# The last projections and the first kept pair by block products, in the second pass of a three-pass fp32 layer

## The chip, the cores and the metric

The kernel runs on one core of a Trainium2 chip. The metric is the device time in microseconds; of several executions the median counts. The profile is one further execution, recorded by the hardware profiler. Engines are named as in the profile: PE is the matrix engine (TensorE), DVE the vector engine, ACT the scalar engine, POOL GpSimd, SP the engine whose queue issues most DMAs.

## What is computed

The reference is a "macaron" layer on x of 4 x 1024 x 1024, all in fp32: a feed-forward part, an attention part, the same feed-forward part again, each on the layer-normed x and added to it.

```python
x = x + 0.5 * ffn(layernorm(x))
x = x + attention(layernorm(x))
x = x + 0.5 * ffn(layernorm(x))
...
def ffn(x):                                   # x: 4096 tokens of 1024
    dots = softmax(x @ centroids.T / 0.1)     # 64 clusters
    hits = dots > 0.01
    dense = x @ weight.T + bias
    return where(any(hits, axis=1)[:, None] & any(hits, axis=0)[assignments][None, :], dense, 0)
```

The attention mixes the heads of one token only (`bsdh,bseh->bsde`), and the repeat of k and v over the heads lets the 32 query heads be summed to 8, so that q, k and v together are 768 columns. Which columns of a feed-forward output count is known only when all tokens have been through the gate (`dots`), so each feed-forward part is finished one pass later than it is begun.

## The kernel before, in words

The 4096 tokens are 32 tiles of 128 rows (`NT = 32`). There are three passes over the tiles, each written out by hand in the order of the program; every engine takes its own instructions in that order. The first pass does the first feed-forward product. The second pass, the loop `for s in range(NT + 5)` at the middle of the file, adds it, does the attention, and begins the second feed-forward part. The third does the rest of the products and writes the output.

**The second pass as a pipeline.** Step s works on several tiles at once: it projects tile s to q, k and v, does the attention's small products of tile b = s - 2, adds the attention's result of g = s - 3 on POOL (`second_added`) and norms that tile for the second feed-forward part, transposes f = s - 4 into xT, and gates a = s - 5 (`gate_2`, eight matmuls of 320 columns that give the last 256 output columns and the 64 gate logits). On DVE the order within a step is: the maximum and the subtraction of the scores (L886, L888), the thresholds of the gates (`gated`, four small instructions per tile, L408 to L414), the transpose and the sums of the exponentials (L897 to L910), the moments of tile g (`moments`, `normed`, L162 to L173), and then whatever evicts the products of this step, and the attention's output o (L929, L931).

**Block products.** `project` multiplies one tile by 768 columns of wqkv: 2 x 8 matmuls of 384 columns. `project_two` does the same for two tiles with Strassen's scheme in Winograd's form: seven products of 4 matmuls of 384 columns where the plain way takes eight. The steps of PAIRED = range(4, 30) use it; a generator, `two`, is advanced five products in the even step and two in the odd one. Its sums of weights (`qts`) lie in the first 768 columns of wc, where W.T of the feed-forward part lay in the first pass; W.T was saved to DRAM (`wtd`) and is brought back by four DMAs from SP, blocks 0 and 1 in step 29, blocks 2 and 3 in step 30. Tiles 0 to 3, 30 and 31 use `project`.

The feed-forward products of a pair of tiles are `winograd`: seven products in the order 1, 5, 2, 6, 7, 3, 4. Product 6 is accumulated **onto** product 1's PSUM bank (`onto=u`, L303), and product 4 onto product 7's (`onto=y`, L326). Product 1's bank is also read by DVE before that, since product 1 alone, with the bias, belongs to one quarter of the output:

```python
        u = prod(1, a11, w11)
        add(ca[:, 0], u, b1)
...
        prod(6, s2, t2, onto=u)
```

In the same way `add(cb[:, 1], y, ca[:, 1])` reads product 7 ahead of product 4. The sums of weights `ts` lie in wqkv (`blocks(wqkv)`), so that they can be written only when the projections are done; the sums of tokens `ss` are made by POOL.

The last six tiles (`KEPT`, 26 to 31) stay on chip for the third pass, and some of their products are done in the second pass's last five steps, which have no projection. Before the change tiles 26 and 27 are done by `rest` in steps 32 and 33, one tile per step (2 x 8 matmuls of 384 columns, each half evicted by DVE with the bias), with two of the four weight sums on DVE after each; tiles 28 and 29 are done by `winograd` in steps 34 and 35. In step 34 its first three products are called ahead of `moments`.

**The gates' book.** `gate_2(a)` leaves the logits in es[a]; at the end of the step ACT takes the exponential; `gates_used` in a later step empties es and applies the thresholds. In a paired odd step two tiles are gated, a and f (a + 1), except where the next step is not paired. In a step that is not paired the last lines are `elif has(a) and a not in es: gate_2(a)`.

PSUM holds four banks for products and transposes (`bank`, tag mm), and four that hold the scores and the attention's output in turn (tag att).

Of the kernel before, what the change touches and what calls it, by code (L numbers as in the profile page):

```python
# [33 lines left out]
KEPT = 6  # L34
LAST = 2 * HALF, (EMB + NCL) // 2 - HALF
GATED = range(8, 28)
PAIRED = range(4, 30)
WARM = 16
ROWS = 26

# [2 lines left out]
def kernel(  # L43
# [39 lines left out]
    nc = tc.nc  # L83
    xf = x.flatten_outer_dims()
    of = out.flatten_outer_dims()
    NT = xf.shape[0] // P
# [20 lines left out]
    for base, sign in ((0, 1), (HKV - 1, -1)):  # L107
        nc.gpsimd.affine_select(
            out=tq,
            in_=tq,  # L110
# [9 lines left out]
    wc = const.tile([P, KT, EMB + NCL], F32, name="wc")  # L120
# [14 lines left out]
    xt, dt_, xT = {}, {}, {}  # L135
# [79 lines left out]
    def ffn_part(src, i, dst, name, biased=True):  # L215


        lo, hi = PARTS[i]
        p = product(src, wc, lo, hi, f"ff_{name}_{i}")
        hi = min(hi, EMB)  # L220
        if biased:
            nc.vector.tensor_tensor(dst[:, lo:hi], p[:, : hi - lo], brow[:, lo:hi], ALU.add)
        else:
            nc.scalar.copy(dst[:, lo:hi], p[:, : hi - lo])
        return p[:, hi - lo : hi - lo + NCL] if i == 2 else None

    def rest(t):

        for i in range(2):
            ffn_part(xT[t], i, dt_[t], f"3_{t}")  # L230
        del xT[t]

    def blocks(wts, lo=0, n=HALF):

        return [
            wts[:, 4 * i : 4 * i + 4, lo + h * n : lo + (h + 1) * n] for i in (0, 1) for h in (0, 1)
        ]

    def weight_sums(ws, ts, engines):

        w11, w12, w21, w22 = ws
        t1, t2, t3, t4 = ts
        sums = (t1, w12, w11), (t2, w22, t1), (t3, w22, w12), (t4, w21, t2)
        for engine, (o, p, q) in zip(engines, sums):
            engine.tensor_tensor(o, p, q, ALU.subtract)
            yield
# [214 lines left out]
    def first_added(t):  # L461
        masked(dt_[t], t, 0, mask)
        nc.gpsimd.tensor_tensor(xt[t], xt[t], dt_.pop(t), ALU.add)  # L463
# [6 lines left out]
    with (  # L470
# [5 lines left out]
        ts = [stage.tile([P, 4, HALF], F32, tag=f"ws{i}", name=f"ws{i}") for i in range(4)]  # L476
# [286 lines left out]
    with (  # L763
# [129 lines left out]
        def weighted(s, t, between=lambda: None):  # L893


            st = attn.tile([P, NBLK, 4, D], F32, tag="stt", name=f"stt{t}")
            nc.vector.transpose(  # L897
                st.rearrange("p b t d -> p (b t d)"), s.rearrange("p b t e -> p (b t e)")
            )
            between()  # L900
            sm = small.tile([P, 2, 4, 4], F32, tag="asm", name=f"asm{t}")
            nc.vector.tensor_reduce(
                sm.rearrange("p m i t -> p i m t"),
                s.rearrange("p (i m) t e -> p i m t e", m=2),
                AX.X,
                ALU.add,
            )
            rs = small.tile([P, D], F32, tag="rs", bufs=3, name=f"rs{t}")
            nc.vector.transpose(rs, sm.rearrange("p m i t -> p (m i t)"))
            nc.vector.reciprocal(rs, rs)  # L910
            return st, rs
# [44 lines left out]
        def has(t):  # L956
            return 0 <= t < NT
# [13 lines left out]
        def gate_2(a):  # L971
            if a not in dt_:
                dt_[a] = row(f"d3_{a}")
            es[a] = gate(ffn_part(xT[a], 2, dt_[a], f"3_{a}", biased=a >= FIRST_KEPT), a, 1)

        def gates_used():
            for a in sorted(es):
                gated(es.pop(a), a, 1)
                if a < FIRST_KEPT:
                    store_2(a)  # L980

        for s in range(NT + 5):
            b, g, f, a = s - 2, s - 3, s - 4, s - 5
            paired, odd = s in PAIRED, s % 2 == 1
            if has(s + 4):
                load_2(s + 4)
            for i in {PAIRED.stop - 1: (0, 1), PAIRED.stop: (2, 3)}.get(s, ()):

                nc.sync.dma_start(out=blocks(wc)[i], in_=wtd[i])
            if has(b):  # L990
                sc = scores(qkv[b][0], kd.pop(b), b)
            if has(b):
                nc.scalar.activation(sc, sc, AF.Exp, scale=QK_SCALE)
            if paired:
                if not odd:
                    two = project_two(s, s + 1, ss2)
                next(two)
            if has(s + 1) and s + 1 not in xT2:
                xT2[s + 1] = transposed(xn2.pop(s + 1), f"2_{s + 1}")
            if has(s - 1):  # L1000
                kd[s - 1] = keys(qkv[s - 1][0], s - 1)
            if has(g):
                second_added(ot.pop(g), rs.pop(g), g)
            if g >= 0 and g < FIRST_KEPT:
                nc.gpsimd.dma_start(out=y2[g], in_=xt[g])
            if odd or not paired:
                gates_used()
            if 3 <= s <= 4:
                next(qsums)
            if has(s + 2):  # L1010
                normal = sums_normed(xt[s + 2], f"2_{s + 2}")
                next(normal)
            if paired and not odd:
                next(two)
            if has(b):
                st, rs[b] = weighted(sc, b, lambda: next(two) if paired and odd else None)
            if paired and not odd:
                first_added(s + 3)
                next(two)
            if has(s + 2):  # L1020
                xn2[s + 2] = next(normal)
            if paired and not odd:
                next(two)
            if paired and odd and s + 1 in PAIRED:
                gate_2(a)
                xT[f] = transposed(xn3.pop(f), f"3_{f}")
            if paired and (not odd or s + 1 not in PAIRED):
                fo = attend(st, qkv.pop(b)[1], b)
            if s == NT + 2:
                dt_[a] = row(f"d3_{a}")  # L1030
                steps = winograd(s - 6, s - 5, ss, ts, None, 3)
                for _ in range(3):
                    next(steps)
            if has(g):
                mv = moments(xt[g], f"3_{g}")

            def between():
                if has(s + 3) and s + 3 in dt_:
                    first_added(s + 3)
                if has(g):  # L1040
                    xn3[g] = normed(xt[g], mv, f"3_{g}")

            if paired:
                if not odd:
                    next(two)
                between()
            elif has(s):
                flat[s] = project(xT2.pop(s), s, between)
            else:
                between()  # L1050
                k = s - NT
                if k < 2:
                    rest(s - 6)
                    if k == 0:
                        sums = weight_sums(blocks(wc), ts, [nc.vector] * 4)
                    for _ in range(2):
                        next(sums)
                if k > 2:
                    load_xT(k - 3)
                if 2 <= k < 4:  # L1060
                    for _ in range(1 if k == 2 else 3):
                        next(steps)
            if paired and odd:
                qkv[s] = rearranged(flat.pop(s), s)
            if has(b) and b in qkv:
                fo = attend(st, qkv.pop(b)[1], b)
            if s in flat:
                qkv[s] = rearranged(flat.pop(s), s)
            if has(b):
                ot[b] = returned(fo, b)  # L1070
            if has(s - 1):
                qkv[s - 1] = (qkv[s - 1][0], values(qkv[s - 1][1], s - 1))
            if has(f) and f in xn3:
                xT[f] = transposed(xn3.pop(f), f"3_{f}")
            if odd and s + 1 in PAIRED:
                xT2[s + 2] = transposed(xn2.pop(s + 2), f"2_{s + 2}")
                ss2 = token_sums(xT2, s + 1, s + 2, "2q")
            if 1 <= s <= 3:

                for _ in range(2 if s == 1 else 1):  # L1080
                    next(held[s // 2])
                i = {1: NT - 4, 3: NT - 2}.get(s)
                for i in (i, i + 1) if i else ():
                    nc.sync.dma_start(out=d1[i], in_=dt_.pop(i))
            if s == 1:
                next(qsums)
            if s == NT + 1:
                ss = token_sums(xT, f - 1, f, 2)
                asg = load_assigned()
            if s == NT + 3:  # L1090
                hot = one_hot(asg)
            if paired:
                if odd:
                    gate_2(f if s + 1 in PAIRED else a)
            elif has(a) and a not in es:
                gate_2(a)
            for i in sorted(es) if odd or not paired else ():
                es[i] = gate_exp(es[i], i, 1)
# [118 lines left out]
```

## Time and profile before

| what | value |
|---|---|
| median of three runs | 1326.33 us (1325.13 to 1327.94) |
| the profiled execution, its own time | 1330.44 us |
| span in that profile | 1328.7 us |
| PE busy | 1304.5 us, 98% |
| DVE, ACT, POOL busy | 875.3, 495.3, 583.3 us |
| granted PE clock | 0.995 |

Every fp32 matmul of the program leaves two records in the profile (16 matmuls of a tile's projection are 32 records), and records overlap, so a stage's length is read from the starts of the merged lines and not from the mean duration of a record. In the timelines below a line gives start, length, engine, source line, operation, output and inputs, count, and in brackets the idle time before it and what ended it. A step of the second pass begins on PE with its scores (sc, L877).

### The profile page before, as it was taken

How to read it: one execution, taken by the hardware profiler on the slowest of the kernel's cores; microseconds unless marked ns; L12 is line 12 of the kernel's file. 1: busy time of each engine (PE TensorE's matmuls, PEld its weight loads, DVE VectorE, ACT ScalarE, POOL GpSimd, SP SyncE). 2: the span in 40 equal slices, each digit the busy share in tenths (PEclk: the TensorE clock that was granted, in tenths of full speed). 3: DMA queues.
4: the chain of work that ended last, by engine and by line, in shares of the span. 5: the costliest groups of instructions: out<-in, count | busy, mean ns of one | idle time of the engine just before them, and what ended most of it. 6: DMA issues, size and time to landing. Idle time of an engine off the chain costs nothing.

```text
span 1328.7 us, 22771 instructions
## 1 busy us (share of the span) xinstructions
PE 1304.5 (98%) x8726; PEld 842.6 (63%) x8726; DVE 875.3 (66%) x1789; ACT 495.3 (37%) x821; POOL 583.3 (44%) x448
## 2 busy tenths in 40 slices
PE   8998899999999999999999999999999999999998
PEld 7664577676776665666666666666666655555554
DVE  4574555655546458788888888878867448555556
ACT  4342132332310335666666666666653200000000
POOL 2631123412112238666666666666632336634440
PEclk8999999999999999999999999999999999999999
DMA  8376766677524055566666656656551346755532
GB/s 294 75 155 147 157 148 140 148 178 189 118 95 183 20 160 179 153 192 197 199 185 198 199 165 198 198 186 187 158 171 29 97 140 218 250 194 176 177 117 81
DMA packets 296301, 214.25 MB, mean 161 GB/s; under 512 B 240064, under 2 KB 255168, under 8 KB 296192
## 3 DMA queue, kind: packets, MB, share of 16 engines
q1 hardware_dynamic: 278240, 164.78, 45.4%
q0 software_dynamic: 8736, 30.68, 6.3%
q10 hardware_dynamic: 9216, 17.33, 3.6%
q8 instruction: 69, 1.13, 0.4%
q14 instruction: 40, 0.33, 0.1%
HBM read 127.77 MB, written 84.96 MB: 160 GB/s over the span
## 4 chain that ended last, share of the span: by engine, by line
PE 89%; DVE 5%; issue 2%; ACT 2%; DMA 1%; SPq 1%; ACTq 0%; DVEq 0%
PE st L284 38%; PE qs L801 18%; PE ff L212 16%; PE tp L205 4%; PE la L348 4%; PE pq L212 4%; PE sc L877 2%; PE po L919 2%; DVE d L275 1%; DVE bn L162 1%; SPq L490 1%; PE tpw L558 1%; DMA scd<-sc 0%; DVE best L414 0%; DMA x<-in_L_attn_x_dram 0%
## 5 line engine op out<-in xcount | busy, mean ns | idle before, releaser
L212 PE MATMUL ff<-wc,xT 128*128 128x320 f32 (+1 forms) x768 | 218.7, 439 | 1.0 <-ACT xT L206 0.6
L212 PEld LDWEIGHTS ff<-wc,xT 128*128 128x128 f32 x768 | 144.1, 191 | 63.8 <-issue 1.2
L284 PE MATMUL st<-wc,xT 128*128 128x384 f32 x496 | 170.4, 487 | 0.0
L257 POOL TENSOR_TENSOR ts<-xT 128x512 f32<-128x512 f32 x31 | 42.2, 1361 | 291.3 <-DVE xT L509 95.3
L275 DVE TENSOR_TENSOR d<-st,d 128x384 f32<-128x384 f32 x157 | 85.9, 549 | 106.6 <-PE st L284 105.5
L857 POOL TENSOR_TENSOR kd<-qk,tmask 128x1024 f32<-128x1024 f32 x32 | 60.6, 1893 | 162.5 <-DMA qk<-qkvd 159.5
L284 PEld LDWEIGHTS st<-wc,xT 128*128 128x128 f32 x496 | 93.3, 191 | 60.3 <-issue 1.2
L284 PE MATMUL st<-ws,ts 128*128 128x384 f32 x384 | 131.2, 487 | 0.1
L284 PE MATMUL st<-wqkv,ts 128*128 128x384 f32 x360 | 121.3, 486 | 0.0
L162 DVE BATCH_NORM_STATS2 bn<-x 128x6 f32<-128x512 f32 x132 | 84.2, 680 | 34.9 <-DMA x<-in_L_attn_x_dram 33.3
L801 PE MATMUL qs<-wc,ts_2q 128*128 128x384 f32 x312 | 106.2, 490 | 0.0
L463 POOL TENSOR_TENSOR x<-x,d 128x1024 f32<-128x1024 f32 x32 | 75.4, 2356 | 68.9 <-DVE d L452 52.8
L452 DVE SCALAR_TENSOR_TENSOR d<-d,qsel,mask 128x1024 f32<-128x1024 f32 (+2 forms) x68 | 104.0, 1530 | 0.1
L284 PEld LDWEIGHTS st<-wqkv,ts 128*128 128x128 f32 x360 | 68.3, 190 | 48.1 <-issue 0.8
L284 PEld LDWEIGHTS st<-ws,ts 128*128 128x128 f32 x384 | 71.1, 190 | 43.4 <-issue 1.6
L165 ACT ACTIVATE mv<-mv,eps 128x1 f32<-128x1 f32 x66 | 19.4, 295 | 205.0 <-DVE mv L164 198.4
L284 PE MATMUL st<-wc,ts 128*128 128x384 f32 x248 | 86.7, 494 | 4.0 <-DVE d L275 4.0
L206 ACT COPY xT<-tp 128x512 f32<-128x512 f32 x138 | 73.2, 581 | 32.2 <-PE tp L205 31.3
L801 PEld LDWEIGHTS qs<-wc,ts_2q 128*128 128x128 f32 x312 | 58.2, 190 | 40.5 <-issue 2.6
L275 DVE TENSOR_TENSOR d<-st,brow 128x384 f32<-128x384 f32 x93 | 51.2, 550 | 43.3 <-PE st L284 43.1
L948 POOL TENSOR_TENSOR x<-x,ot 128x1024 f32<-128x1024 f32 x32 | 78.0, 2439 | 2.5
L509 DVE STREAM_TRANSPOSE xT<-xb 128x1024 f32<-128x1024 f32 x27 | 33.6, 1245 | 67.2 <-ACT xb L505 52.9
(143 smaller groups left out, 2294.2 us busy)
## 6 DMA issues: line engine op xcount, KB each, us to landing
x<-in_L_attn_x_dram SPq DMA_DIRECT2D x64, 512.0 KB, 4.4
d<-d SPq DMA_DIRECT2D x64, 512.0 KB, 4.4
out_dram<-x ACTq DMA_DIRECT2D x30, 512.0 KB, 4.7
xb<-in_L_attn_x_dram SPq DMA_DIRECT2D x108, 128.0 KB, 4.9
y<-x POOLq DMA_DIRECT2D x26, 512.0 KB, 3.1
xTd<-xT POOLq DMA_DIRECT2D x26, 512.0 KB, 5.5
xT<-xTd SPq DMA_DIRECT2D x26, 512.0 KB, 5.0
x<-y SPq DMA_DIRECT2D x26, 512.0 KB, 5.2
```

The source lines that it names most:

```text
L162: nc.vector.bn_stats(st[:, i, :], src[:, i * 512 : (i + 1) * 512])
L205: nc.tensor.transpose(tp[:, j, :], xn[:, k * P : (k + 1) * P], ident)
L206: nc.scalar.copy(t_[:, 4 * h : 4 * h + 4, :], tp)
L212: nc.tensor.matmul(p, src[:, k, :], wts[:, k, lo:hi], start=(k == 0), stop=(k == KT - 1))
L275: nc.vector.tensor_tensor(out, ps, other, ALU.add)
L284: nc.tensor.matmul(ps, src[:, k, :], wts[:, k, :], start=(k == 0 and onto is None), stop=(k == 3), skip_group_check=onto is not None,)
L348: nc.tensor.matmul(ps, src[:, k, :], wts[:, k, :], start=(k == 0 and onto is None), stop=(k == 3), skip_group_check=onto is not None,)
L452: nc.vector.scalar_tensor_tensor(d[:, sl], d[:, sl], qsel[which][:, t : t + 1], mask[:, sl], ALU.mult, ALU.mult)
L463: nc.gpsimd.tensor_tensor(xt[t], xt[t], dt_.pop(t), ALU.add)
L801: nc.tensor.matmul(ps, src[:, k, :], wts[:, k, :], start=(k == 0 and onto is None), stop=(k == 3), skip_group_check=onto is not None,)
L857: nc.gpsimd.tensor_tensor(kd, qk[:, :, D:].unsqueeze(2).to_broadcast([P, NBLK, 4, D]), tmask.unsqueeze(1).unsqueeze(3).to_broadcast([P, NB ...
L948: nc.gpsimd.tensor_tensor(xv, xv, ov, ALU.add)
```

## The change

PAIRED is extended to range(4, 32): tiles 30 and 31 are projected by `project_two`. Steps 29 and 31 thereby get the form of the other odd steps. W.T comes back in step 31: blocks 1 and 0 at its start, blocks 3 and 2 after the sums of the exponentials. `rest` is deleted; tiles 26 and 27 are done by `winograd`, four products in step 32 and three in step 33, after `moments` and `normed`. Their sums of tokens, and the first two sums of weights, are put at the end of step 31; the other two sums of weights follow the four products in step 32.

```diff
-PAIRED = range(4, 30)
+PAIRED = range(4, 32)
...
-    def rest(t):
-
-        for i in range(2):
-            ffn_part(xT[t], i, dt_[t], f"3_{t}")
-        del xT[t]
...
+        def returns(*some):
+
+            for i in some:
+                nc.sync.dma_start(out=blocks(wc)[i], in_=wtd[i])
...
-            for i in {PAIRED.stop - 1: (0, 1), PAIRED.stop: (2, 3)}.get(s, ()):
-
-                nc.sync.dma_start(out=blocks(wc)[i], in_=wtd[i])
+            if s == NT - 1:
+                returns(1, 0)
...
                 st, rs[b] = weighted(sc, b, lambda: next(two) if paired and odd else None)
+            if s == NT - 1:
+                returns(3, 2)
             if paired and not odd:
-                first_added(s + 3)
+                if has(s + 3):
+                    first_added(s + 3)
...
-            if paired and odd and s + 1 in PAIRED:
+            if paired and odd:
                 gate_2(a)
                 xT[f] = transposed(xn3.pop(f), f"3_{f}")
-            if paired and (not odd or s + 1 not in PAIRED):
+            if paired and not odd:
                 fo = attend(st, qkv.pop(b)[1], b)
...
                 between()
                 k = s - NT
                 if k < 2:
-                    rest(s - 6)
-                    if k == 0:
-                        sums = weight_sums(blocks(wc), ts, [nc.vector] * 4)
+                    for _ in range(4 - k):
+                        next(steps)
+                if k == 0:
                     for _ in range(2):
                         next(sums)
...
+            if s == NT - 1:
+                ss = token_sums(xT, f - 1, f, 2)
+                steps = winograd(f - 1, f, ss, ts, None, 3)
+                sums = weight_sums(blocks(wc), ts, [nc.vector] * 4)
+                for _ in range(2):
+                    next(sums)
...
             if paired:
                 if odd:
-                    gate_2(f if s + 1 in PAIRED else a)
+                    gate_2(f)
             elif has(a) and a not in es:
                 gate_2(a)
```

## The prediction

> **What bounds the kernel now.** First the page's busy times and the waits of PE, then the order of PE and of DVE in the steps that the change touches. The page, and PE's waits from 900 to 1130 us (us in total, times, longest):
>
> ```profile
> PE 1304.5 (98%) x8726; PEld 842.6 (63%) x8726; DVE 875.3 (66%) x1789; ACT 495.3 (37%) x821; POOL 583.3 (44%) x448
> ```
> ```profile
> PE tp L205 <- ACT xT L206: 1.8, 1, 1.8
> PE ff L212 <- DVE d L275: 0.5, 1, 0.5
> ```
>
> PE works through; after 1060 us it has no wait at all. So what PE gains or loses in steps 29 to 35 reaches the end in full. PE's timeline of steps 29 to 32:
>
> ```profile
> 952.01 2.79 PE L801 MATMUL qs<-wc,xT 128*128 128x384 f32 x8
> ...
> 964.50 0.66 PE L205 MATMUL tp<-ident,xn 128*128 128x128 f32 x4 [1.78 <-ACT xT L206]
> 964.99 10.58 PE L212 MATMUL pq<-wqkv,xT 128*128 128x384 f32 x32
> ...
> 999.68 1.07 PE L877 MATMUL sc<-kd,qk 32*32 32x128 f32 x64
> 1000.68 10.59 PE L212 MATMUL ff<-wc,xT 128*128 128x384 f32 x32
> 1011.20 1.07 PE L919 MATMUL po<-stt,vt 32*32 32x128 f32 x64
> 1012.19 1.09 PE L205 MATMUL tp<-ident,xn 128*128 128x128 f32 x8
> 1013.12 4.47 PE L212 MATMUL ff<-wc,xT 128*128 128x320 f32 x16
> ```
>
> Prices from starts: a projection or a tile of `rest` takes 10.5 us, one product of four matmuls a quarter of that, 2.63; a gate 4.4 (1013.12 to 1017.53), scores 1.0, attention's output 1.0, a transpose 0.93. Now DVE in the same step 32:
>
> ```profile
> 1000.78 1.23 DVE L886 TENSOR_REDUCE amx<-sc 128x32 f32<-128x1024 f32 x1
> ...
> 1007.35 1.22 DVE L162 BATCH_NORM_STATS2 bn<-x 128x6 f32<-128x512 f32 x2
> ...
> 1009.50 0.55 DVE L222 TENSOR_TENSOR d<-ff,brow 128x384 f32<-128x384 f32 x1
> 1011.30 0.56 DVE L222 TENSOR_TENSOR d<-ff,brow 128x384 f32<-128x384 f32 x1 [1.25 <-PE ff L212]
> 1011.78 1.75 DVE L245 TENSOR_TENSOR wqkv<-wc 128x1536 f32<-128x1536 f32 x1
> ```
>
> The reader is to see the lag: the first half of tile 26 is ready on PE at 1005.9, but DVE evicts it at 1009.50, since the scores, thresholds, exponentials and moments stand ahead of it. The eviction ends at 1010.05, 10.4 us after the step's start at 999.68. In step 33 it is the same (1027.90 against 1017.53). Before the change that lag costs nothing: the other half goes to another bank.
>
> **What the Trainium skill says.** "TensorE: Matmul & The Clock Gate", Step-by-step: what each phase is for: matmuls stay in program order, only weight loads are pulled ahead; so one matmul that waits holds all behind it. The trace agrees: in the first pass PE sat 4.04 us at 134.50 with its next products queued. The same page, Architectural detail: ACT and DVE are strict FIFO. The DVE lines above agree: the eviction came 3.6 us after its bank was ready. "PSUM — Partial Sum Buffer", The four PSUM rules: a partial sum may be read in the middle of an accumulation group if the read is synchronised. That is `u` and `y` here, and the trace shows its price, at a product 4:
>
> ```profile
> 112.72 4.41 PE L284 MATMUL st<-ws,xT 128*128 128x384 f32 x8 [2.32 <-DVE d L275]
> ```
>
> "DMA: Bandwidth & Descriptors", Issuing engines are not separate DMA queues: SP's and POOL's transfers share 16 engines, which matters for W.T below.
>
> **The change part by part.** T31, T32, T33 are the starts of a step's scores.
>
> *Projections.* 64 records become 56: 21.0 us become 7 x 2.63 = 18.4, so -2.6 on PE. Step 29 becomes a plain odd step, whose model, step 27 (912.58 to 931.29), has no stall; the 1.8 us before 964.50 go. Nothing else is late there.
>
> *Tiles 26 and 27.* Eight products become seven: -2.6.
>
> *A second gate of tile 27.* This is not in the words of the change, but in its bookkeeping. Step 31 is now a paired odd step, so it gates a = 26 and f = 27. Step 32 isn't paired: its `gates_used` empties es, and then `a not in es` holds for a = 27, and gate_2(27) runs again. Before, gates were counted 44 x 16 = 704 records (32 tiles here, 12 in the first pass); now 720. The result is the same, since the maximum of best is taken twice. It costs +4.4 on PE, on the path.
>
> *Sum on PE alone.* -2.6 - 2.6 - 1.8 + 4.4 = -2.6. By steps: 18.7 (29, as 27), 16.2 (30, as 28), 16.9 (31, as 27 less two transposes), 17.85 (32: four products for one tile of `rest`), 15.1 (33) make 84.75 where 947.46 to 1035.28 took 87.8: -3.1. I take **-2.9**.
>
> *Wait 1: product 6 onto u, step 32.* PE is ready for it at T32 + 1.0 + 3 x 2.6 = +8.8. `add(ca, u, b1)` has to have read u before. Its place on DVE is that of the old eviction, behind `moments`, so it ends at +10.4 if DVE is no later than before: 1.6 us of wait at the least. But DVE is later. (a) Two tiles' thresholds instead of one, +0.8 (1003.19 to 1003.99). (b) Two weight sums, 1.75 each, now stand on DVE at the end of step 31, ahead of the second gate's eviction. In step 29 tile 26's sum for the moments came from POOL at T29 + 11.8; with the same timing for tile 28, DVE does its moments, then o (2.0), the transpose of v (0.45), and both sums until about T31 + 20.1, while step 32 begins at about T31 + 17.5: +2.6. Some 0.4 of that goes into DVE's idle times (0.46 and 0.36 in the old step 32). End +13.4, wait **4.6**; bounds 1.6 (no lateness) and 6.2 (tile 29's sum comes from POOL at +12 because its transfers queue behind W.T, and its moments to the eviction take 2.9 more). Behind the waiting product stand attention's output of tile 30, a transpose, the gate.
>
> *Wait 2: scores of tile 31.* Three evictions, the sums t3 and t4 (3.5) and then o are now in one stretch on DVE behind product 6; o frees the bank of the scores 7.2 us after product 6 ends (3 x 0.55 + 3.5 + 2.0), while PE needs 1.0 + 0.9 + 4.4 = 6.3 to get there. Wait **0.6**, bounds 0 and 1.
>
> *Wait 3: product 4 onto y, step 33.* Ready at T33 + 1.0 + 2 x 2.6 = +6.2; `add(cb, y, ca)` ends at +10.4 as the old eviction did in step 33. Wait **4.3**; bounds 3.5 (DVE ahead by 0.7) and 5.
>
> *Wait 4: product 4 onto y of the projection, step 31.* In an odd step a transpose stood between products 7 and 4; step 31 has none. The eviction ended 0.6 us after product 7 (951.90 in step 29, PE at 951.2). **0.6**, bounds 0 and 0.8.
>
> *W.T back.* Four DMAs of 768 KB. On SP blocks 1 and 0 pass ahead of the store of tile 31's q, k, v, and blocks 3 and 2 ahead of its reload, of od and of ot of tile 29; POOL's stores of two gated tiles (1.3 MB) share the engines. In step 29 the issue came at T29 + 6.6 (954.05) and landing took 4.9 to 7.9. All four with the store are 3.5 MB; at the 390 GB/s of the trace's best slices there 9 us, so +15.7; with POOL's stores +19. t1 wants its blocks at +16.6, t2 wants block 3 at +18.3, PE wants w21 at T32 + 6. Cost taken: nothing. Its cover is the rest of step 31; if that is gone, DVE waits for t2 and every us goes into wait 1.
>
> *Off the path.* POOL: two times four token sums, 1.27 each, in steps 29 and 31; POOL is busy 19.1 of the 50 us from 950 to 1000. Eight more evictions of 0.55 on DVE: counted in wait 2. Steps 34 and on are as before.
>
> *Sum.* -2.9 + 4.6 + 0.6 + 4.3 + 0.6 = **+7.2**. The profiled execution took 1330.44 (span 1328.7, 1.7 around it), 4.1 above the median of the runs; the difference is carried to the median: 1326.3 + 7.2 = **1333.5**. The bounds of the waits give -3.1 + 5.1 = +2.0 to -2.7 + 13.0 = +10.3: 1328.3 to 1336.6.
>
> **Rivals.** (R1) *Only PE's records count.* If DVE reads u and y in time, by T32 + 8.8 and T33 + 6.2, the waits are nil and the sum is -2.9: **1323.4**, faster. For it: the same generator in steps 34 and 35 runs with one wait of 0.46. Against it: there the first three products stand ahead of `moments`; in steps 32 and 33 they stand behind it, and the old evictions show 10.4. Chance 0.05. (R2) *Small waits.* One of the two waits is much smaller, because DVE has caught up: 1.6 for wait 1, 2 for wait 3, none else: +0.7, **1327.0**. Chance 0.07. (R3) *W.T is late.* Block 3 lands some 5 us after DVE asks for it, or tile 29's attention, whose transfers stand behind it, does: +12, **1338.5**. For it: step 29's landing of 7.9 with two blocks only. Against it: 390 GB/s is seen in the slices that moved them. Chance 0.13. That the change does not do its work can be excluded for the products; for the gate it does more than its words say.
>
> **How the numbers follow.** The forecast has 0.75. R1 and R2 lie under 1328.5; of R3 half lies above 1338.5; so 0.05 + 0.07 + 0.065 are left out of the range **1328.5 to 1338.5**. A measurement of this kernel tells about 0.2% (2.7 us) from no change: faster 0.05 (R1), same 0.07 (R2), slower 0.88.
>
> **What would show it.** 720 records of the 320-column gate (two gates of tile 27); seven products per pair in steps 30, 31 and 32, 33; no stall at the transposes of step 30. PE waits on DVE's d (L275 then) of some 4 us each at an st<-...,ts product in step 32 and an st<-...,xT product in step 33, each ended by an eviction that stands right behind bn. DVE's wait for DMA wc<-wtd near nil, else R3. The prediction is wrong if PE has no wait there, or if gates count 704.

## The result, and the profile after

| | before | after |
|---|---|---|
| median of four runs each, same chip, us | 1326.43 | 1342.9 |
| lowest to highest | 1325.13 to 1327.94 | 1341.88 to 1345.05 |
| profiled execution, its span | 1330.44, 1328.7 | 1342.64, 1340.9 |
| granted PE clock in it | 0.995 | 0.991 |

The change makes the kernel slower, by a ratio of 1.0127 [1.0107, 1.0148]: **+16.5 us** where +7.2 was forecast. All ratios here and below are of fast executions; two slow ones, of 2737.78 us with product 1 ahead and of 2252.26 us in (d) below, are left out. The page after, its busy times and two groups of instructions:

```profile
PE 1309.9 (98%) x8726; PEld 845.1 (63%) x8726; DVE 881.3 (66%) x1804; ACT 495.6 (37%) x823; POOL 592.2 (44%) x456
...
L212 PE MATMUL ff<-wc,xT 128*128 128x320 f32 x720 | 201.6, 433 | 1.1 <-ACT xT L206 0.6
...
L278 PE MATMUL st<-wqkv,ts 128*128 128x384 f32 x384 | 132.3, 494 | 7.8 <-DVE d L269 7.8
```

The gate has 720 records and PE as many as before (8726): what the block products save in number, 16 records, the second gate of tile 27 adds. Yet PE's busy time grew by 5.4 us. PE's waits from 930 to 1070 us (total, times, longest):

```profile
PE st L278 <- DVE d L269: 13.2, 2, 7.8
PE qs L795 <- DVE qkv L828: 0.6, 1, 0.6
PE sc L871 <- DVE o L925: 0.6, 1, 0.6
PE st L278 <- DMA wc<-wtd: 0.6, 1, 0.6
```

The first three lines are the forecast's four waits, the last is one on W.T. (The eviction's line L275 is L269 now, and other lines moved too.) Where they stand, in PE's timeline of steps 31 to 33:

```profile
980.25 2.85 PE L795 MATMUL qs<-wc,xT 128*128 128x384 f32 x8 [0.65 <-DVE qkv L828]
...
993.72 1.07 PE L871 MATMUL sc<-kd,qk 32*32 32x128 f32 x64
...
997.40 2.74 PE L278 MATMUL st<-wqkv,ts 128*128 128x384 f32 x8
1000.74 2.85 PE L278 MATMUL st<-wc,xT 128*128 128x384 f32 x8 [0.60 <-DMA wc<-wtd]
1011.35 5.46 PE L278 MATMUL st<-wqkv,ts 128*128 128x384 f32 x8 [7.76 <-DVE d L269]
...
1024.00 1.06 PE L871 MATMUL sc<-kd,qk 32*32 32x128 f32 x64 [0.64 <-DVE o L925]
...
...
1035.83 5.46 PE L278 MATMUL st<-wqkv,xT 128*128 128x384 f32 x8 [5.41 <-DVE d L269]
```

Products 6 (1011.35) and 4 (1035.83) wait for DVE to have read the bank that they accumulate onto. And each of the two, once it runs, takes 5.46 us in place of 2.74. Busy time by stretch tells why (length; busy us and count of PE, PEld, DVE, ACT, POOL; granted clock; DMA share; GB/s):

```profile
1003.50:1011.35 7.85, 0.09 (x2) 0.04 (x1) 6.21 (x16) 2.75 (x4) 3.39 (x3) 0.72 0.05 17
1011.35:1016.80 5.45, 5.45 (x18) 2.55 (x24) 0.51 (x1) 0.71 (x1) 0.00 (x0) 0.50 0.02 3
1016.80:1024.00 7.20, 6.57 (x89) 4.63 (x89) 7.01 (x10) 2.36 (x3) 0.00 (x0) 0.97 0.00 0
1035.80:1041.30 5.50, 5.47 (x20) 2.60 (x28) 0.56 (x1) 0.84 (x1) 0.00 (x0) 0.51 0.00 0
```

During the wait the granted clock falls (0.72 in the mean of the long wait), the next product runs wholly at 0.50, and then it is near 1 again. The two products, 2.72 us longer each, are the added busy time.

**Where the time went.** The steps' lengths, from the starts of their scores on PE (the last one to the first product of step 34):

| step | 29 | 30 | 31 | 32 | 33 | sum |
|---|---|---|---|---|---|---|
| before | 13.60 | 20.77 | 17.85 | 17.85 | 17.75 | 87.8 |
| after | 18.86 | 16.17 | 17.96 | 30.28 | 23.46 | 106.7 |

From there to the end both take 293.4 us. So **+18.9** lies in this window: waits 0.65 + 0.60 + 7.76 + 0.64 + 5.41 = 15.1, two products at half clock 2 x 2.72 = 5.4, the attention's output right after one 0.2, and a remainder of -1.8, which is put down to PE's own work. This stretch, from the scores of step 29 to the first product of step 34, is called the window. It is compared below, since the time ahead of it, which the edits leave alone, differs by some us between executions; it starts 6.7 us later in the profile of before, whose execution took 4 us more than the median.

**Why DVE was so late in step 32.** DVE's timeline of after:

```profile
993.55 1.81 DVE L239 TENSOR_TENSOR wqkv<-wc 128x1536 f32<-128x1536 f32 x1
998.05 1.76 DVE L239 TENSOR_TENSOR wqkv<-wc,wqkv 128x1536 f32<-128x1536 f32 x1 [2.69 <-DMA wc<-wtd]
...
1000.51 1.22 DVE L880 TENSOR_REDUCE amx<-sc 128x32 f32<-128x1024 f32 x1
...
1008.43 1.29 DVE L162 BATCH_NORM_STATS2 bn<-x 128x6 f32<-128x512 f32 x2 [1.00 <-POOL x L942]
1010.65 0.55 DVE L269 TENSOR_TENSOR d<-st,brow 128x384 f32<-128x384 f32 x1
```

The second weight sum, t2, waits 2.69 us for W.T's block 3, so the scores' maximum (1000.51) begins 6.8 us after the scores, not 1.1 as before. In parallel tile 29's sum comes late from POOL, 14.7 us after the scores, so the moments (1008.43) wait another 1.00; the eviction of product 1 stands right behind them. The DMA issues on SP's queue say why tile 29 is late:

```profile
983.52 1.27 SPq L979 DMA_DIRECT2D wc<-wtd  x2
984.89 0.56 SPq L807 DMA_DIRECT2D qkvd<-qkv  x1
985.55 1.38 SPq L979 DMA_DIRECT2D wc<-wtd  x2
992.31 0.38 SPq L839 DMA_DIRECT2D qk<-qkvd  x1
992.73 7.30 SPq L845 DMA_DIRECT2D v<-qkvd  x4
1000.08 0.45 SPq L929 DMA_DIRECT2D od<-o  x1
```

The issue of tile 31's v took 7.30 us behind W.T (step 29's, ahead of W.T, 2.05), and the attention result of tile 29 stood behind it. W.T's four blocks took 5.0 to 14.4 us from issue to landing, 9.7 in the median, against 4.9 to 7.9, median 5.6, before. That v's issue is slow because of W.T is inferred from the order and from other cases: behind four blocks it took 7.22 in another run too, behind two 4.67 and 4.17 us (the runs with t2 on POOL and with W.T earlier, below), ahead of W.T 2.05.

### The profile page after: what moved, and what is told of

It reads as the page before. It is cut to its first block, busy times and chain, and to the rows that moved or that the text cites. A ratio compares the mean times of both kernels' runs of the same rounds, so it can differ in the third digit from the quotient of the medians.

```text
span 1340.9 us, 22800 instructions
## 1 busy us (share of the span) xinstructions
PE 1309.9 (98%) x8726; PEld 845.1 (63%) x8726; DVE 881.3 (66%) x1804; ACT 495.6 (37%) x823; POOL 592.2 (44%) x456
## 4 chain that ended last, share of the span: by engine, by line
PE 91%; DMA 4%; DVE 3%; ACT 1%; SPq 0%; POOL 0%; issue 0%; DVEq 0%; ACTq 0%; POOLq 0%
PE st L278 40%; PE qs L795 20%; PE ff L212 14%; PE la L342 6%; PE tp L205 4%; PE pq L212 2%; PE sc L871 2%; PE po L913 2%; DMA x<-in_L_attn_x_dram 1%; DMA wc<-wtd 1%; DMA scd<-sc 1%; DVE bn L162 1%; DVE d L269 1%; PE tpw L552 1%; DMA od<-o 1%
## 5 line engine op out<-in xcount | busy, mean ns | idle before, releaser
L212 PE MATMUL ff<-wc,xT 128*128 128x320 f32 x720 | 201.6, 433 | 1.1 <-ACT xT L206 0.6
L278 PE MATMUL st<-wc,xT 128*128 128x384 f32 x512 | 175.9, 487 | 0.6 <-DMA wc<-wtd 0.6
L212 PEld LDWEIGHTS ff<-wc,xT 128*128 128x128 f32 x720 | 134.9, 190 | 57.1 <-ACT xT L206 1.2
L269 DVE TENSOR_TENSOR d<-st,d 128x384 f32<-128x384 f32 x162 | 88.8, 550 | 111.6 <-PE st L278 110.3
L278 PE MATMUL st<-wqkv,ts 128*128 128x384 f32 x384 | 132.3, 494 | 7.8 <-DVE d L269 7.8
L795 PE MATMUL qs<-wc,ts_2q 128*128 128x384 f32 x336 | 114.4, 490 | 0.0
L278 PEld LDWEIGHTS st<-wqkv,ts 128*128 128x128 f32 x384 | 73.8, 193 | 60.3 <-issue 11.1
L278 PE MATMUL st<-wc,ts 128*128 128x384 f32 x256 | 89.6, 494 | 2.4 <-DVE d L269 2.4
L795 PEld LDWEIGHTS qs<-wc,ts_2q 128*128 128x128 f32 x336 | 62.7, 190 | 43.6 <-issue 2.8
L269 DVE TENSOR_TENSOR d<-st,brow 128x384 f32<-128x384 f32 x96 | 52.9, 551 | 46.8 <-PE st L278 46.8
L795 PE MATMUL qs<-wqkv,xT 128*128 128x384 f32 x224 | 78.3, 492 | 0.0
```

The source lines that it names most:

```text
L212: nc.tensor.matmul(p, src[:, k, :], wts[:, k, lo:hi], start=(k == 0), stop=(k == KT - 1))
L269: nc.vector.tensor_tensor(out, ps, other, ALU.add)
L278: nc.tensor.matmul(ps, src[:, k, :], wts[:, k, :], start=(k == 0 and onto is None), stop=(k == 3), skip_group_check=onto is not None,)
L795: nc.tensor.matmul(ps, src[:, k, :], wts[:, k, :], start=(k == 0 and onto is None), stop=(k == 3), skip_group_check=onto is not None,)
```

## The experiments

A run's ratio is to the kernel before, measured together with it. The medians of before differ by up to 7 us from one such group of measurements to the next, so ratios and windows are compared. The window is 87.8 us before and 106.7 after, in one profiled execution each. Edits are against the kernel after unless another is named. The theory is that the two long waits and the half clock behind them make the loss; "+16.5" is to be taken away or reproduced in parts.

**One gate of tile 27** (the repeated gate is left out; the result doesn't need it).

```diff
-            elif has(a) and a not in es:
+            elif has(a) and a not in es and s != NT:
```

> The changed kernel with the second gate of tile 27 left out in step 32 (the first one, in step 31, stays). Theory of the record: the gate's 16 records are on PE's path, so the time falls by 4.4 us, from 1342.9 to 1338.5. Rival (the gate is only a filling): in the profile after the change o of tile 30 ends on DVE at 1023.7 and the scores of tile 31 wait for it by 0.64 us; without the gate PE gets there 4.4 us sooner, waits about 5.0 us for the same o, and the next product runs at half clock (+2.7): 1341 to 1345, no gain.

Ratio 1.0117 [1.0092, 1.0142], window 104.8: 4.4 us less of PE work bring 1.9 in the window and nothing beyond the interval in the ratio. PE's timeline of this run:

```profile
1025.98 1.51 PE L871 MATMUL sc<-kd,qk 32*32 32x128 f32 x64 [5.18 <-DVE o L925]
```

The gate only filled a wait: DVE's chain behind product 6 (evictions, t3, t4, o) sets when tile 31's scores may start, at 0.64 with the gate and 5.18 without.

**Product 1 ahead of the scores' chain.** Product 1 in step 32, and product 7 in step 33, are called right after the exponentials are issued, so that their evictions are no longer behind `moments`; PE's order of the products stays the same.

```diff
+            if NT <= s < NT + 2:
+                next(steps)
...
-                    for _ in range(4 - k):
+                    for _ in range(3 - k):
```

> The changed kernel with only DVE's order changed: product 1 of tiles 26 and 27 (with its eviction) is called right after the scores of tile 30, and product 7 right after the scores of tile 31, ahead of the gates' thresholds, the exponentials' sums and the moments; PE's order is as it was. Theory (the two long waits are the evictions' places on DVE): both waits of PE on d, 7.8 and 5.4 us, go below 1 us and the 2 x 2.7 us of half clock go; but o of tile 30 then comes late behind t3 and t4, with a new wait of some 6 us at the scores of tile 31: about 1342.9 - 12.2 - 5.4 + 6 + 2.7 = 1334. Rival (PE waits for late W.T or late tokens, and the eviction only ended last): the wait of step 32 stays above 4 us and the time above 1339.

Ratio 1.0040 [1.0023, 1.0056], window 91.6: 15 us of the 18.9 are gone, with both waits. PE's timeline, the next in line:

```profile
1014.09 0.66 PE L205 MATMUL tp<-ident,xn 128*128 128x128 f32 x4 [3.14 <-DVE d L269]
...
1015.14 6.26 PE L212 MATMUL ff<-wc,xT 128*128 128x320 f32 x16 [0.40 <-DVE d L269]
```

The transpose waits 3.14 us for a bank of the products that DVE frees late, and the gate behind it runs in part at half clock (6.26 us, not 4.4; the granted clock was 0.50 from 1017.0 to 1018.5). The scores' wait that was expected did not come: o ended at 1020.84, and PE, held up by these two, came to the scores only at 1021.34.

**Idle transposes in the waits.** 60 transposes of the identity ahead of product 6 and 38 ahead of product 4, into a bank that nobody reads: work that is not the layer's, to keep PE busy.

```diff
+        def fill(n):
+            if name == 3 and a == FIRST_KEPT:
+                f = bank(f"fill_{n}")
+                for _ in range(n):
+                    nc.tensor.transpose(f[:, :P], ident, ident)
...
+        fill(60)
...
+        fill(38)
```

> The changed kernel with idle work put on PE: 60 transposes of the identity (some 7 us) ahead of product 6 in step 32 and 38 (some 4.4 us) ahead of product 4 in step 33, into a bank that nobody reads; nothing else. Theory (the clock granted to PE falls to a half while it waits, and the product after the wait pays for it): both products take 2.7 instead of 5.46 us, and with what follows earlier, 1342.9 - 5.4 = 1337.5. Rival (the product is slow for another reason, an operand or a bank that is shared): they stay at 5.46 us and the time at 1342 to 1344.

Ratio 1.0070 [1.0048, 1.0092], window 99.6, 7.1 less than after. PE's timeline and the stretch of product 6:

```profile
1014.00 2.82 PE L278 MATMUL st<-wqkv,ts 128*128 128x384 f32 x8 [1.28 <-DVE d L269]
```
```profile
1014.00:1016.90 2.90, 2.90 (x26) 1.56 (x41) 0.56 (x2) 0.72 (x1) 0.00 (x0) 1.00 0.00 0
```

With work of no use the kernel is faster: the products run at clock 1.00, in 2.82 and 2.85 us instead of 5.46. So the half clock is a price of the wait, not of the product. Its share is 5.5 of the 7.1 us (5.3 in the two products, 0.2 in the attention's output). The rest is not the clock's: product 4 stands 10.4 us after the scores of step 33 instead of 11.8, since tile 30's sum came sooner from POOL in this execution and the moments did not wait for it, and product 6 came 0.4 us sooner; the scores' wait took 0.2 back.

**W.T earlier, by itself.** Blocks 1 and 0 in step 30, after its fourth product.

```diff
-            if s == NT - 1:
-                returns(1, 0)
...
+            if s == NT - 2:
+                returns(1, 0)
```

> The changed kernel with blocks 1 and 0 of W.T brought back in step 30, after that step's fourth product, instead of at the start of step 31. Theory (the W.T blocks land late: DVE waited 2.7 us for block 3, PE 0.6 us for w21, and od and ot of tile 29 queued behind them): those waits go, the wait of step 32 falls from 7.8 to some 5 us: 1342.9 - 3.3 = 1339.6. Rival (tile 29's sum from POOL, not W.T, sets when the eviction comes): the wait of step 32 stays within 1 us and the time at 1342 to 1343.

Ratio 1.0127 [1.0095, 1.0159], window 103.8. The theory missed: DVE and PE wait for W.T no more, and tile 29's sum is done 10.7 us after the scores (14.7 in after), yet wait 1 is 7.39 us. The rival's number came, but not for its reason, since DVE no longer waits for that sum. (Two of the 2.9 us that the window is shorter come from the products behind the waits, which took 4.44 and 4.53 us here and 5.46 in after.) DVE's and POOL's timelines of step 32:

```profile
1005.94 2.06 DVE L408 SCALAR_TENSOR_TENSOR best<-ge,gsm,best 128x64 f32<-128x64 f32 x1
```
```profile
1005.58 2.34 POOL L942 TENSOR_TENSOR x<-x,ot 128x1024 f32<-128x1024 f32 x1
```

The threshold's instruction takes 0.28 us in the median; here it ends when POOL's sum of tile 29 ends. The weight sum t2 likewise took 2.71 in place of 1.76, and POOL's token sums 2.8 in place of 1.27. So DVE, which no longer waits, lost some 3.3 us of its own beside POOL before it reached the moments, 13.6 us after the scores. The Trainium skill, "SBUF — State Buffer", Who interferes with whom, says that a DVE instruction with two SBUF inputs contends with a GpSimd instruction that reads SBUF, and that the port pair they share is an exclusive lock; these lines agree.

**Each half of the change alone.** First only the kept pair by `winograd`, from the kernel before, with the sums at the end of step 31:

```diff
-                    rest(s - 6)
...
+                    for _ in range(4 - k):
+                        next(steps)
...
+            if s == NT - 1:
+                ss = token_sums(xT, f - 1, f, 2)
+                steps = winograd(f - 1, f, ss, ts, None, 3)
+                sums = weight_sums(blocks(wc), ts, [nc.vector] * 4)
+                for _ in range(2):
+                    next(sums)
```

> The kernel before with one part of the change alone: tiles 26 and 27 by winograd in steps 32 and 33 at the change's places, their sums of tokens and t1, t2 at the end of step 31; the projections of tiles 30 and 31 as before, W.T back in steps 29 and 30 as before, one gate of tile 27. Theory (the evictions' places on DVE make the loss; W.T and the second gate add to it): -2.6 for the product, waits of 2 to 3 us at product 6 and of some 4 us at product 4, both products at half clock (+1.7 to +2.7 each), scores of tile 31 about 0.6: +7 to +9 us against before, 1334 to 1337. Rival (late W.T and the second gate make the waits): waits under 1 us, 1323 to 1327.

Ratio 1.0060 [1.0040, 1.0080], window 98.3 (+10.4). W.T is back two steps earlier here, and DVE is late all the same:

```profile
1015.43 4.32 PE L284 MATMUL st<-wqkv,ts 128*128 128x384 f32 x8 [3.41 <-DVE d L275]
...
1037.36 5.31 PE L284 MATMUL st<-wqkv,xT 128*128 128x384 f32 x8 [4.00 <-DVE d L275]
```

These two waits are near the 4.6 and 4.3 of the forecast, where W.T and the second gate are out of the way. Then only the projections, with `rest` in place of `winograd`:

```diff
-                returns(3, 2)
+                returns(2, 3)
...
-                    for _ in range(4 - k):
-                        next(steps)
-                if k == 0:
+                    rest(s - 6)
+                    if k == 0:
+                        sums = weight_sums(blocks(wc), ts, [nc.vector] * 4)
```

> The changed kernel with the other part alone: tiles 30 and 31 by project_two and W.T back in step 31 (blocks 1 and 0, then 2 and 3, since rest wants block 2 first), tiles 26 and 27 by rest as before, the second gate of tile 27 kept. Theory: -2.6 for the product, -1.8 for the stall of step 30, +4.4 for the gate, +0.6 at product 4 of the projection, and 0 to 4 us if block 2 lands after rest asks for it, with half clock if that wait is over 2 us: 0 to +6 against before, 1327 to 1333. Rival (the paired steps 30 and 31 themselves are the loss): above 1335.

Ratio 1.0033 [1.0022, 1.0044], window 94.0 (+6.2), although the product and the stall that it saves should pay for its second gate (-2.6 - 1.8 + 4.4):

```profile
1019.79 6.27 PE L212 MATMUL ff<-wc,xT 128*128 128x320 f32 x16 [3.54 <-DVE d L222]
```

Here the repeated gate waits for a bank and runs in part at half clock (0.50 from 1022 to 1024). By the windows the halves make 10.4 + 6.2 = 16.6 of the 18.9, by the ratios 0.6 + 0.33 of 1.27 per cent: each half loses by waits of its own, and they add up only roughly.

**t2 on POOL** (`[nc.vector, nc.gpsimd, nc.vector, nc.vector]` as engines of the sums), so that DVE needn't wait for block 3; then the same with W.T earlier. Each of the two was executed once, so they have windows but no ratio.

> The changed kernel with the weight sum t2 on POOL instead of DVE, nothing else: DVE no longer waits 2.7 us for W.T's block 3 and is spared 1.75 us. Theory A (DVE's lateness from t2 makes the step 32 wait longer than predicted): the wait of 7.8 us falls to some 3.5 us. Theory B (tile 29's sum from POOL, behind od and ot that stand behind W.T's transfers, bounds it as well; in the changed kernel DVE idles 1.0 us for it): the wait falls by about 1 us only, to 6 to 7.5 us.

> As e12_t2_pool, with blocks 1 and 0 of W.T back in step 30. Theory A: as e12_t2_pool, about 3.5 us of wait in step 32. Theory B (two causes side by side, either of which keeps the wait long): only with both taken away does the wait fall, to 3.5 to 5.5 us.

Windows 106.0 and 104.2. In the first wait 1 is 7.54; DVE's moments now wait for POOL:

```profile
1011.47 1.29 DVE L162 BATCH_NORM_STATS2 bn<-x 128x6 f32<-128x512 f32 x2 [3.94 <-POOL x L942]
```

DVE was ready for them 10.2 us after the scores, but tile 29's sum was done after 14.2, about as late as in after (14.7), since its transfer still stood behind v on SP. So block 3 and tile 29's sum are two causes in parallel, and mending the first alone brings nothing. With W.T earlier as well wait 1 is 5.93, just above the 3.5 to 5.5 that theory B expected. DVE lost 3.3 us there beside POOL (L408 took 2.31 and 1.50), and POOL, which now has t2 (3.44 us) ahead of tile 29's sum, finished that sum 12.0 us after the scores; DVE waited only 0.17 us for it. So the two were late together, and this run doesn't tell them apart.

**In search of a version that is faster.** (a) One gate; product 1 ahead, as above; products 5, 2, 6 ahead of `moments`; tile 29's moments after the attention; product 7 ahead in step 33; t2 to t4 on POOL. (b) The same with W.T earlier. (c) As (a), but the steps from 32 gate tile f instead of a, to have a gate's work in step 32 without repeating one:

```diff
-            elif has(a) and a not in es and s != NT:
+            elif s < NT and has(a):
...
+            elif s >= NT and has(f):
+                gate_2(f)
```

(d) As (c), with tile 29's moments after its predecessor's transposes, and t3 on POOL in step 32.

> The changed kernel mended: one gate of tile 27; product 1 of tiles 26 and 27 right after the scores of step 32 and its products 5, 2, 6 ahead of the moments; product 7 right after the scores of step 33; the moments of tile 29 after attention's output of tile 30; t2, t3, t4 on POOL (t2 and t3 at the end of step 31). Theory: -2.6 - 2.6 - 1.8 stay, +0.6 (product 4 of the projection), +0.6 (w21), +1 to +2 (o of tile 30): -4 to -5 against before, some 1322. Rival (DVE, POOL and the transfers have no room in these steps for the block products, in whatever order): a new wait of 3 us or more somewhere, with half clock behind it, 1326 or above.

> As e9_best, with blocks 1 and 0 of W.T back in step 30 after its fourth product. Theory: the wait for w21 (0.6) goes and od of tile 29 comes sooner: 0.5 to 2 us under e9_best. Rival (only the order of DVE and POOL matters): the same as e9_best within 0.5 us.

> e9_best with a gate in the place of the one left out: from step 32 on each step gates f = s - 4, the tile it has just transposed, instead of a = s - 5, so step 32 gates tile 28 and step 36 none. Theory (the scores of tile 31 wait 3.0 us for o in e9_best because nothing stands between; a gate that is due anyway covers that wait and its half clock): the wait at those scores goes, 4.4 us of gate leave the end; small waits of 0.3 us for the copies of xT at the gates: 3 to 5 us under before, ratio 0.996 to 0.998. Rival (the gate only moves, and waits for its own transposes and banks): the same as before within 1 us.

> e11_gates_ahead with two of its orders changed: the moments and the norm of tile 29 after the transpose of tile 28 (in e11 ACT's copy of that transpose stood behind the norm, and PE waited 6.8 us for it), and t3 on POOL in step 32, behind tile 29's sum, instead of ahead of it. Theory (with evictions, copies and gates in place, what is left of the change is its saved products): no wait over 1.5 us in steps 32 and 33; steps 29 to 33 take about 88 us, as before, and the end is reached 3 us sooner because a gate has moved forward: 2 to 4 us under before, ratio 0.997 to 0.9985. Rival (steps 32 and 33 have no room on DVE): a new wait of 3 us or more, ratio 1.000 or above.

Ratios: (a) 0.9989 [0.9977, 1.0001], (b) 0.9993 [0.9984, 1.0003], (c) 1.0061 [1.0042, 1.0079], (d) 1.0002 [0.9984, 1.0019]. None beats the kernel before beyond its interval. In (a), whose window of 88.0 us equals that of before, the scores wait for o, and DVE stands beside POOL's weight sum, which ends at 1012.07; PE's and DVE's timelines:

```profile
1019.18 1.52 PE L871 MATMUL sc<-kd,qk 32*32 32x128 f32 x64 [3.02 <-DVE o L925]
```
```profile
1009.12 3.03 DVE L408 SCALAR_TENSOR_TENSOR best<-ge,gsm,best 128x64 f32<-128x64 f32 x1
```

In (c) the gate waits 6.82 us for the copy of its transposes, which stood behind tile 29's norm on ACT: an order of mine, mended in (d), where instead the gate of tile 29 waits 2.93 for DVE (the profile names o) and takes 6.26. In none of the four did the work saved on PE reach the end: a new wait for DVE or ACT, with half clock behind it, took it up. That no order at all can win is not shown.

## Why the prediction was right in kind and wrong in size

- **The mechanism holds.** The sign, the places of both long waits, the eviction right behind `moments`, the second gate of tile 27 and the waits of 0.6 each at the projection's product 4 (0.65) and at tile 31's scores (0.64) came as told; the second with some luck, since its own sum, 7.2 less 6.3, gives 0.9 and not 0.6. Steps 29 and 30 took 18.86 and 16.17 for 18.7 and 16.2, and their stall went. Removing the cause takes 15 of 18.9 us away (product 1 ahead). R1, only PE's records count, has fallen.
- **The step that failed most is the price of a product, "2.63", taken for the products behind the waits as well**: the half clock behind a wait was put at nothing. It cost +5.4 in the two products and +0.2 behind them. It was to be seen in the line that the prediction itself quoted from the first pass: 4.41 us for a product behind a wait of 2.32; I read the wait and not the 4.41. The other wait that I named, 4.04 at 134.50, has a product of 4.42 behind it. The Trainium skill states it too ("TensorE: Matmul & The Clock Gate", Part 1: The HAM clock gate: an idle window of about 3.4 us drops the clock to half). The idle transposes confirm the half clock by experiment; the 3.4 us do not fit the shorter waits of these traces, as the last section shows.
- **Wait 1 was mis-sized**, 4.6 where 7.76 was measured, beyond the bound of 6.2. The second step that failed is "W.T back: cost taken: nothing". The estimate of its landing, 15.7 us after the start of step 31 or 19 with POOL's stores, rested on 390 GB/s and an issue at +6.6; the issue came at +7.8, the 4.8 MB moved at 330 GB/s in the mean, and block 3 was there at +22.3. It held DVE by 2.69 us, and tile 29's transfers stood behind a queue on SP that takes 7.30 us for v. The upper bound had the right mechanism, tile 29's sum behind W.T, but put it 12 us after the scores; it came after 14.7. R3 named both causes, as alternatives; both came. With t2 off DVE alone the wait is 7.54. With W.T earlier it is 7.39, and there a third cause that the prediction did not have, DVE's loss beside POOL, sets it; with both it is 5.93, from that loss and POOL's added t2 together.
- **Wait 3**: 4.3 forecast, 5.41 measured; the moments of step 33 waited 1.26 us for POOL's sum of tile 30, which "as the old eviction did" left out. With the idle transposes, where the moments did not wait, product 4 came 1.4 us sooner. That accounts for the difference of 1.1.
- **Adding the gate's 4.4 to the path counted it wrongly.** It fills the scores' wait, so taking it away brings little (1.9 in the window). My sum was right only with the gate in place; as a price of the gate it was not one.
- **PE alone**: -2.9 forecast, -1.8 left over in the sum. Without their waits and the half clock, steps 29, 31, 32 and 33 are each 0.2 to 0.5 us longer than forecast; why was not followed up.

The terms: clock +5.6, wait 1 +3.2, PE's own work +1.1, wait 3 +1.1, W.T's wait on PE +0.6 come to 11.6, which takes +7.2 to the +18.9 of the window. The two profiled executions differ by 12.2, since that of before reached the window 6.7 us later; it lay 4.0 above its median, and that of after 0.3 below, so the medians differ by 16.5. What makes the time ahead of the window vary was not looked into; it is the 2.4 us between 18.9 and 16.5.

## What to carry to other kernels

A saved matmul is worth its time only if the accumulations that replace it don't have to wait for a reader; before one accumulates onto a bank that a vector engine reads in between, put that read where that engine comes first, and not behind a chain that hangs on a transfer. Price a wait of the matrix engine together with the work behind it at half clock, and look in the profile of before for how long the instructions after its waits took: here waits of 2.9 us or more always cost it, and waits of about 2.3 us in eight traces of fourteen. A transfer that is moved is priced with everything behind it in its queue, and an instruction moved to POOL with the DVE instructions that it will hold up.

## What the runs showed of the hardware

- **The half clock can follow a wait shorter than the 3.4 us cited above, and not every time.** In all traces, from 40 us on, work behind waits of 0.7 to 2.15 us kept its length. Behind waits of 2.93 us and more a product took 3.6 to 5.5 us in place of 2.74 to 2.85, and a gate 6.3 to 6.8 in place of 4.5. In between it is not settled by the length: one product of the first pass waits 2.31 or 2.32 us in every trace, and it took 4.2 to 4.5 us in eight (before and after among them) and 2.85 in six. PE's timeline of (a), for the line of before that the prediction shows:

```profile
112.38 2.85 PE L278 MATMUL st<-ws,xT 128*128 128x384 f32 x8 [2.31 <-DVE d L269]
```

In before the granted clock was 1.00 during this wait, 0.94 in the first 1.3 us of the product and 0.50 after that; in (a) it stayed 1.00. So in before it fell only when PE was at work again. What decides it was not tried.
- **A small DVE instruction can last as long as POOL's beside it**: the threshold's last one takes 0.28 us in the median, 2.06 and 3.03 beside POOL's sums, ending with them. The trace of before has one of 3.03 too, at 316.90 beside a weight sum on POOL, so this could have been seen.
- **The issue of DMAs took longer behind large transfers**: four issues for v took 7.30 us on SP behind 3 MB of W.T, 2.05 without.
